# The third pass of a graph layer: rows on GpSimd, squares split between two engines, the copy a step later

## The chip, the cores and the metric

The kernel runs on one core of a Trainium2 chip. Its engines work in parallel, each through its own list of instructions in order: TensorE (PE in the profile; PEld is its loading of weights), VectorE (DVE), ScalarE (ACT), GpSimd (POOL), and SyncE (SP), which only issues transfers here. Semaphores order the engines among each other. The metric is the time of one execution on the device in microseconds (us); the time given is the median of several runs.

## The reference

Two layers follow each other on 16 graphs of 1024 nodes with 128 features. Layer 0 is a gated graph network of four steps, added to its input and normalized. Layer 1 thins out the adjacency matrix row by row, passes three times over all graphs, and joins what the passes leave:

```python
def _sage(x, adj, Wr, Wx, b, mf):
    deg = jnp.clip(jnp.sum(adj, axis=-1, keepdims=True), 1.0, None)
    agg = jnp.einsum('bij,bjd->bid', adj, x) / deg
    out = agg @ Wr + x @ Wx + b
    nrm = jnp.maximum(jnp.linalg.norm(out, axis=-1, keepdims=True), NORM_EPS)
    return out / nrm * mf[..., None]
...
h1 = _bn(jax.nn.relu(_sage(x, adj_d, Wr1, Wx1, b1, mf)), g1, be1)
h2 = _bn(jax.nn.relu(_sage(h1, adj_d, Wr2, Wx2, b2, mf)), g2, be2)
h3 = _bn(jax.nn.relu(_sage(h2, adj_d, Wr3, Wx3, b3, mf)), g3, be3)
xc = jnp.concatenate([h1, h2, h3], axis=-1) * mf[..., None]
return (xc @ Wl + bl) * mf[..., None]
```

`_bn` normalizes each feature over all nodes of all graphs, so a pass has to end before the next can use its result. The change lies in the third pass: `out` for `h3`, its row norm, the division, the mask and `relu`, and the sums of squares that `_bn` needs.

## The kernel before

The first stages (gated network, thinning, first and second pass) are outside the change. When the third pass starts, the aggregates `agg` of `h2` are already in memory (`s_ag`), and so are the turned rows of `h2` (`s_rt`); the third pass has no large matrix product any more.

`Sage.third` (L1850) goes through 32 units: 16 graphs, two halves `f` of 512 nodes each. A unit holds four blocks of 128 nodes by 128 features. The order of every engine's list is written out by hand (`manual_schedule`): what the loop emits first stands first in its engine's list. Step `i` of the loop emits work of several units, so that engines need not wait for each other within a step:

- SyncE: at the first half of each graph, `load_layer` for the next graph: 512 KB of aggregates (`q_agi`), 512 KB of turned rows (`q_xt`), and a small `s_rho`; three buffers each.
- TensorE: `out_next` of unit i (L1769): four products into `q_oa` (aggregates by weights), four into `q_ob` (rows by two weight matrices side by side), four small ones that add the bias. Then `turned` of unit i-3 (L1422): four transposes of the rows `s_r` into a PSUM tile `s_tr`. All three PSUM tiles have two buffers, which fills the PSUM.
- VectorE: `rows` of unit i-2 (L1407): lower bound, reciprocal and mask on a 128x4 tile of norms `ss`, then one 128x512 instruction, `max(o, 0) * ss`, into `s_r`. Then `bn_stats` of unit i-4 on `r3`. Then, of unit i, the add of `q_ob` into `s_o` (L1396), and the add of the other half of `q_ob` into `s_acc` (L1889).
- ScalarE, all of unit i but the last: four scalings of `q_oa` by the reciprocal degrees into `s_o` (L1393), four squares with an accumulator that gives each row's sum of squares (L1403, each followed by a read of the accumulator), a square root (L1404), and the copy of unit i-3's turned block from PSUM into `r3` (L1891).

Within a step, the squares read what the add on VectorE wrote, and that add reads what the scaling on ScalarE wrote. `s_o`, `s_r` and the loaded tiles have three buffers, `ss` has four.

At the start of step 8 stands `flagged` (L1995): VectorE reduces a table of checks (`bad`, 128x161) to a column, TensorE multiplies that by a column of ones into a PSUM tile taken from `s_tr`, and VectorE compares the product with 0.5. All of it stands ahead of step 8's own work in each list. At step 16 the flag is loaded into a register. It decides, after the whole pass, whether a slow general version has to run.

The third pass is followed by small matrices (`head_weights`) and the last pass, which normalizes and stores.

Of the kernel before, what the change touches and what calls it, by code (L numbers as in the profile page):

```python
# [8 lines left out]
F32 = mybir.dt.float32  # L9
BF = mybir.dt.bfloat16  # L10
# [4 lines left out]
AF = mybir.ActivationFunctionType  # L15
ALU = mybir.AluOpType
# [5 lines left out]
P = 128  # L22
B = 16
N = 1024
C = 128
# [340 lines left out]
class Norm:  # L366
# [5 lines left out]
    def __call__(self, out, rows):  # L372
        nc = self.nc
        st = self.pool.tile([P, NB, 6], F32, name="ln_st")
        mv = self.pool.tile([P, NB, 2], F32, name="ln_mv")
        for k in range(NB):
            nc.vector.bn_stats(st[:, k, :], rows[:, k, :])
        for k in range(NB):
            nc.vector.bn_aggr(mv[:, k, :], st[:, k, :])
        rs = self.pool.tile([P, NB], F32, name="ln_rs")  # L380
        nc.scalar.activation(rs, mv[:, :, 1], AF.Sqrt, bias=self.eps)
        nc.vector.reciprocal(rs, rs)
        for k in range(NB):
            nc.vector.tensor_scalar(out[:, k, :], rows[:, k, :], mv[:, k, 0:1], rs[:, k:k + 1],
                                    op0=ALU.subtract, op1=ALU.mult)


def sage_layers(ctx, tc, cst, adj, mask, not_r, summed, x1, W, vec, Wl, bl, out):
# [37 lines left out]
    def transposed(src, n, evac):  # L426
# [6 lines left out]
        return dst  # L433

    def sage(l, b, rows, ht, at, rd, mf, stats, psa, pso):

        pa = [psa.tile([C, HF], F32, name=f"s_a{f}") for f in range(2)]
# [57 lines left out]
    with ExitStack() as c1:  # L495
# [7 lines left out]
        for b in range(B):  # L503
# [36 lines left out]
            for f in range(2):  # L540
                nc.sync.dma_start(adj_t[b][4 * f:4 * f + 4].rearrange("k p n -> p k n"), at4[f])
            mf = row_tile("s_mf", mask[b])
            sage(0, b, rows, ht, at, rd, mf, stats, psa, pso)
        affine = batch_norm(0, stats)

# [85 lines left out]
class FixPoint:  # L631
# [206 lines left out]
    class Block:  # L838
# [22 lines left out]
        def rows(self, g):  # L861
            fix, nc = self.fix, self.fix.nc
            w = fix.wide.tile([P, N], BF, name="f_w", bufs=2)
            nc.vector.tensor_scalar(w, self.us[g], self.q[:, 2, g:g + 1], 0.5, op0=ALU.not_equal, op1=ALU.subtract)
            nr = fix.wide.tile([P, N], BF, name="f_nr", bufs=5)
            nc.vector.tensor_mul(nr, w, self.a[g])
            nc.sync.dma_start(fix.not_r[self.b0 + g, self.k * P:(self.k + 1) * P, :], nr)
            fix.read_last(self.i, g, nr)
# [341 lines left out]
class Sage:  # L1210
# [188 lines left out]
    def squares(self, o):  # L1399
# [4 lines left out]
        self.nc.scalar.activation(ss, ss, AF.Sqrt)  # L1404
        return ss

    def rows(self, b, f, o, ss):  # L1407
        nc = self.nc
        nc.vector.tensor_scalar(ss, ss, 1e-12, None, op0=ALU.max)  # L1409
        nc.vector.reciprocal(ss, ss)  # L1410
        nc.vector.tensor_mul(ss, ss, self.cst["mask"][:, 4 * f:4 * f + 4, b])
        r = self.wk.tile([P, 4, C], F32, name="s_r")
        sc = ss.rearrange("p (k o) -> p k o", o=1).to_broadcast([P, 4, C])
        nc.vector.scalar_tensor_tensor(r, o, 0.0, sc, op0=ALU.max, op1=ALU.mult)
        return r

    def split(self, f, src, hi, lo, c0=0):
# [363 lines left out]
            nc.tensor.matmul(pb[:, i, 0, :], g["rho"][:, blk], self.r6, start=False, stop=(i % 2 == 1))  # L1781
        g["oa", f], g["ob", f] = pa, pb

    def chain(self, b, f, scalar=False):

        g = self.g[b]
        pb = g.pop(("ob", f))
        g["o", f] = self.scale_rows(b, f, g.pop(("oa", f)), pb[:, :, 0, :], scalar)
        g["ss", f] = self.squares(g["o", f])
        return pb[:, :, 1, :]  # L1790

# [58 lines left out]
    def third(self):  # L1850

        nc, tc = self.nc, self.tc
        with ExitStack() as c:
            pool = lambda name, **k: c.enter_context(tc.tile_pool(name=name, **k))
            self.wk = pool("t_wk", bufs=3)
            self.ps2 = pool("t_ps2", bufs=2, space=PSUM)
            c.enter_context(tc.manual_schedule(engines={ET.PE, ET.DVE, ET.Activation, ET.Pool, ET.SP}))
            last, self.g = self.g[B - 1], {0: self.begun}
            nc.sync.dma_start(self.rt[B - 1, 1], last["rt", 1])
            for f in range(2):  # L1860
                nc.sync.dma_start(self.ag[B - 1, f], last["ag", f])
            units = [(b, f) for b in range(B) for f in range(2)]
            for i in range(len(units) + 4):
                if i == 8:
                    pt = self.ps2.tile([P, 4, P], F32, name="s_tr")
                    flag = flagged(nc, self.one, pt[:1, 0, :1], self.bad)
                if i == 16:
                    self.flag = nc.values_load(flag[0:1, 0:1], min_val=0, max_val=1,
                                               skip_runtime_bounds_check_because="0 or 1 by is_gt")

                if i < len(units):
                    b, f = units[i]
                    if f == 0 and b + 1 < B:
                        self.load_layer(b + 1)
                    self.out_next(b, f, self.ps2)
                if 3 <= i < len(units) + 3:
                    b2, f2 = units[i - 3]
                    pt = self.turned(self.g[b2].pop(("r", f2)), self.ps2)
                if 2 <= i < len(units) + 2:
                    b1, f1 = units[i - 2]  # L1880
                    g = self.g[b1]
                    g["r", f1] = self.rows(b1, f1, g.pop(("o", f1)), g.pop(("ss", f1)))
                if i >= 4:
                    b3, f3 = units[i - 4]
                    nc.vector.bn_stats(self.stats[2][:, 2 * b3 + f3, :], self.r3[:, b3, f3, :])
                if i < len(units):
                    pp = self.chain(b, f, True)
                    acc = self.acc[:, b, 4 * f:4 * f + 4, :]
                    nc.vector.tensor_add(acc, pp, acc)  # L1889
                if 3 <= i < len(units) + 3:  # L1890
                    nc.scalar.copy(self.r3[:, b2, f2, :], pt)  # L1891


    def last(self, r48):
# [97 lines left out]
    nc.vector.scalar_tensor_tensor(junk, a, 0.0, a, op0=ALU.is_gt, op1=ALU.not_equal, accum_out=bad[:, c:c + 1])  # L1992


def flagged(nc, wk, pt, bad):  # L1995

    t = wk.tile([P, 1], F32, name="l_max")
    nc.vector.tensor_reduce(t, bad, axis=AX.X, op=ALU.max)
    nc.vector.tensor_scalar(t, t, 0.0, None, op0=ALU.not_equal)
    col = wk.tile([P, 1], F32, name="l_col")  # L2000
    nc.vector.memset(col, 1.0)
    nc.tensor.matmul(pt, t, col, start=True, stop=True)
    f = wk.tile([1, 1], I32, name="l_flag")
    nc.vector.tensor_scalar(f, pt, 0.5, None, op0=ALU.is_gt)
    return f
# [72 lines left out]
```

## Time and profile before

| what | us |
|---|---|
| median of 3 runs | 2189.92 (2189.5 to 2190.53) |
| the profiled execution | 2193.03 |
| its span, first to last instruction | 2191.1 |
| third pass, first matmul to last `bn_stats` | 1988.22 to 2119.43 |
| in it, from the first to the last add into `s_o` | 1991.49 to 2112.13 = 120.64 |
| busy in those 120.64: TensorE, VectorE, ScalarE, GpSimd | 109.32, 93.19, 91.92, 0.00 |

Lines of the profile name an engine, a line of the kernel (L1396), an operation, the tiles written and read (out<-in), and their shapes. A line of the timeline gives start and duration in us, the number of merged instructions after x, and in brackets the idle time of the engine before it and what ended that. A group of the page gives busy time in all, mean duration in ns, and idle time before the group. An instruction's record can begin before its predecessor's ends; the distance between two starts ("pitch") is then less than the duration.

### The profile page before, as it was taken

How to read it: one execution, taken by the hardware profiler on the slowest of the kernel's cores; microseconds unless marked ns; L12 is line 12 of the kernel's file. 1: busy time of each engine (PE TensorE's matmuls, PEld its weight loads, DVE VectorE, ACT ScalarE, POOL GpSimd, SP SyncE). 2: the span in 40 equal slices, each digit the busy share in tenths (PEclk: the TensorE clock that was granted, in tenths of full speed). 3: DMA queues.
4: the chain of work that ended last, by engine and by line, in shares of the span. 5: the costliest groups of instructions: out<-in, count | busy, mean ns of one | idle time of the engine just before them, and what ended most of it. 6: DMA issues, size and time to landing. Idle time of an engine off the chain costs nothing. (4 is left out here: it accounts for less than half of the span.)

```text
span 2191.1 us, 32979 instructions
## 1 busy us (share of the span) xinstructions
PE 2068.8 (94%) x10217; PEld 1441.4 (66%) x10217; DVE 1838.4 (84%) x4215; ACT 1326.7 (61%) x3238; POOL 1240.4 (57%) x1226
## 2 busy tenths in 40 slices
PE   6999999999999999999999979999999899998977
PEld 4666556666556665556665557777777678887866
DVE  4898998989998889988989978888888767766878
ACT  3657557565666656656575566666666445555757
POOL 4458558467566476575585447777777445551002
PEclk9999999999999999999999989999999999999989
DMA  8348446456455276474383259888888577765505
GB/s 256 76 96 252 90 121 224 86 154 192 92 177 166 77 205 146 97 226 109 83 261 92 68 200 334 306 301 304 302 306 298 178 268 264 268 230 175 156 21 156
DMA packets 233853, 406.13 MB, mean 185 GB/s; under 512 B 79042, under 2 KB 100196, under 8 KB 233668
## 3 DMA queue, kind: packets, MB, share of 16 engines
q1 hardware_dynamic: 187844, 284.37, 39.9%
q0 software_dynamic: 41472, 117.46, 20.2%
q10 hardware_dynamic: 4352, 2.11, 0.4%
q8 instruction: 83, 1.36, 0.3%
q14 instruction: 102, 0.84, 0.1%
HBM read 313.48 MB, written 109.25 MB: 193 GB/s over the span
## 5 line engine op out<-in xcount | busy, mean ns | idle before, releaser
L1104 PE MATMUL h_g<-h_h,h_wh 128*128 128x512 f32 x768 | 396.0, 597 | 3.3 <-DVE h_r L1116 3.3
L1104 PE MATMUL h_g<-h_ms,h_wi 128*128 128x512 f32 x768 | 392.2, 592 | 0.0
L1123 POOL TENSOR_TENSOR h_zh<-h_r,h_h 128x512 f32<-128x512 f32 x126 | 175.4, 1392 | 258.9 <-ACT h_r L1119 255.8
L737 DVE TENSOR_TENSOR_SCAN f_rank<-f_a,f_first,f_pd 128x1024 f16<-128x1024 bf16 x128 | 299.4, 2345 | 4.2
L1092 PE MATMUL h_g<-h_a,h_hi 128*128 128x512 f32 x1024 | 278.8, 413 | 1.3 <-DMA h_a<-in_adj_dram 1.2
L1104 PEld LDWEIGHTS h_g<-h_ms,h_wi 128*128 128x128 f32 x768 | 145.5, 190 | 184.3 <-issue 169.4
L1511 POOL CAST p_b<-p_at 128x512 uint8<-128x512 f32 x256 | 219.7, 880 | 82.8 <-DVE p_at L1503 52.3
L1092 PE MATMUL h_g<-h_a,h_lo 128*128 128x512 f32 x1024 | 262.0, 393 | 0.2 <-DVE h_lo L1030 0.2
L1092 PEld LDWEIGHTS h_g<-h_a,h_hi 128*128 128x128 f32 x1024 | 190.1, 188 | 62.2 <-issue 21.8
L1403 ACT ACTIVATE s_junk<-s_o 128x128 bf16<-128x128 f32 x384 | 114.0, 298 | 169.2 <-DVE s_o L1396 158.3
L1092 PEld LDWEIGHTS h_g<-h_a,h_lo 128*128 128x128 f32 x1024 | 189.7, 188 | 39.0 <-DVE h_lo L1030 1.0
L1104 PEld LDWEIGHTS h_g<-h_h,h_wh 128*128 128x128 f32 x768 | 133.3, 190 | 100.3 <-issue 73.4
L1125 POOL TENSOR_TENSOR h_h<-h_h,h_zh 128x512 f32<-128x512 f32 x126 | 179.0, 1420 | 9.9
L1119 ACT ACTIVATE h_r<-h_r,h_bi 128x512 f32<-128x512 f32 x128 | 92.4, 722 | 151.5 <-DVE h_r L1118 151.4
L1124 POOL TENSOR_TENSOR h_zh<-h_z,h_zh 128x512 f32<-128x512 f32 x126 | 162.5, 1290 | 9.9
L1095 ACT COPY h_ms<-h_g 128x512 f32<-128x512 f32 x128 | 73.9, 577 | 149.7 <-PE h_g L1092 149.6
L910 ACT ACTIVATE f_u<-f_rank,f_q 128x128 f16<-128x128 f16 (+7 forms) x128 | 110.6, 867 | 69.4 <-DVE f_rank L850 69.4
L1778 PE MATMUL q_ob<-s_wxp,q_xt 128*128 128x256 f32 x512 | 125.3, 389 | 3.5 <-DVE s_ss L1409 2.1
L1992 DVE SCALAR_TENSOR_TENSOR p_junk<-p_a 128x1024 bf16<-128x1024 f32 x96 | 126.0, 1312 | 0.0
L887 ACT ACTIVATE f_pd<-f_rank,f_q 128x128 f32<-128x128 f16 x128 | 59.1, 462 | 98.7 <-DVE f_q L701 95.5
L1503 DVE SCALAR_TENSOR_TENSOR p_at<-p_nr,p_u 128x128 fp32r<-128x128 bf16 (+1 forms) x192 | 102.0, 543 | 18.0 <-ACT p_at L1495 14.6
L778 POOL TENSOR_SCALAR_AFFINE_SELECT f_both<-f_both 128x512 bf16<-128x512 bf16 x32 | 20.5, 642 | 165.1 <-DVE f_both L777 165.1
(264 smaller groups left out, 4807.8 us busy)
## 6 DMA issues: line engine op xcount, KB each, us to landing
h_a<-in_adj_dram POOLq DMA_DIRECT2D x128, 512.0 KB, 9.2
p_a<-in_adj_dram SPq DMA_DIRECT2D x96, 512.0 KB
f_a<-in_adj_dram POOLq DMA_DIRECT2D x128, 256.0 KB, 6.5
e_nr<-f_nr SPq DMA_DIRECT2D x128, 256.0 KB
p_nr<-e_nr SPq DMA_DIRECT2D x32, 1024.0 KB
h_test<-in_adj_dram SPq DMA_DIRECT2D x32, 512.0 KB
s_at<-p_b SPq DMA_DIRECT2D x32, 512.0 KB
s_ag<-s_ag SPq DMA_DIRECT2D x64, 256.0 KB
```

Source lines behind the costliest of these rows:

```text
L737: nc.vector.tensor_tensor_scan(out, a, other[:, 0, 0:1].to_broadcast([P, N]), start, op0=ALU.add, op1=ALU.bypass)
L910: nc.scalar.activation(u[:, :n1], rank[:, g, :n1], AF.Abs, bias=q[:, 1, g:g + 1], scale=q[:, 0, g:g + 1])
L1092: nc.tensor.matmul(pm[f], part[:, j, :], st.adj[j][:, half[f]], start=(j == 0 and n == 0), stop=(j == NB - 1 and n == 1))
L1104: nc.tensor.matmul(pg, lhs, rhs, start=(i == 0), stop=(i == len(mm) - 1))
L1123: aid.tensor_tensor(d, r, h, ALU.subtract)
L1124: aid.tensor_tensor(d, z, d, ALU.mult)
L1125: aid.tensor_tensor(h, h, d, ALU.add)
L1403: self.nc.scalar.activation(junk, o[:, i, :], AF.Square, accum_out=ss[:, i:i + 1])
L1503: self.nc.vector.scalar_tensor_tensor(g["at"][:, j, c0:c0 + low], v[:, j, c0:c0 + low], 0.0, pu[:, :low], op0=ALU.is_lt, op1=ALU.is_lt)
L1511: self.nc.gpsimd.tensor_copy(g["b", f][:, j, :], g["at"][:, j, f * HF:(f + 1) * HF].bitcast(F32))
L1778: nc.tensor.matmul(pb[:, i], g["xt"][:, f, blk], self.wxp, start=(i % 2 == 0), stop=False)
L1992: nc.vector.scalar_tensor_tensor(junk, a, 0.0, a, op0=ALU.is_gt, op1=ALU.not_equal, accum_out=bad[:, c:c + 1])
```

## The change

Six things change, all in `third` and its helpers.

1. `rows_by_pool`: the product of `rows` goes from one VectorE instruction to four GpSimd instructions of 128x128, `max(o * ss, 0)`. The three small instructions stay on VectorE. For the last two units `rows` is kept.
2. `shared_squares`: of the four squares, two stay on ScalarE, and two go to VectorE, as products of a tile with itself with an accumulator. They stand behind the add into `s_o` and ahead of the add into `s_acc`. Each pair of sums has its own 128x2 tile, and its own square root on ScalarE, so two roots instead of one.
3. The copy of the turned block is that of the step before (unit i-4), and it stands between ScalarE's scaling and its squares, no longer behind the root.
4. `bn_stats` is accordingly that of unit i-5, and the loop has one step more at its end.
5. The flag: the reduction of `bad` (`any_bad`) stands in step 8 behind the add into `s_o`, the matmul in step 10 behind the transposes, the compare (`flagged`) in step 11. The register is loaded at step 16 as before.
6. The multiplication by `ss` is now ahead of the maximum with zero; `ss` is not negative.

```diff
+    def shared_squares(self, o):
+        nc, small = self.nc, self.small
+        sa, sv = [small.tile([P, 2], F32, name=f"s_ss{i}") for i in range(2)]
+        for i in range(2):
+            junk = small.tile([P, C], BF, name="s_junk")
+            nc.scalar.activation(junk, o[:, i, :], AF.Square, accum_out=sa[:, i:i + 1])
+        for i in range(2):
+            junk = small.tile([P, C], BF, name="s_junk2")
+            nc.vector.scalar_tensor_tensor(junk, o[:, i + 2, :], 1.0, o[:, i + 2, :], op0=ALU.mult, op1=ALU.mult,
+                                           accum_out=sv[:, i:i + 1])
+        ss = small.tile([P, 4], F32, name="s_ss", bufs=4)
+        for i, t in enumerate((sa, sv)):
+            nc.scalar.activation(ss[:, 2 * i:2 * i + 2], t, AF.Sqrt)
+        return ss
...
+    def rows_by_pool(self, b, f, o, ss):
+        nc = self.nc
+        nc.vector.tensor_scalar(ss, ss, 1e-12, None, op0=ALU.max)
+        nc.vector.reciprocal(ss, ss)
+        nc.vector.tensor_mul(ss, ss, self.cst["mask"][:, 4 * f:4 * f + 4, b])
+        r = self.wk.tile([P, 4, C], F32, name="s_r")
+        for i in range(4):
+            nc.gpsimd.tensor_scalar(r[:, i, :], o[:, i, :], ss[:, i:i + 1], 0.0, op0=ALU.mult, op1=ALU.max)
         return r
...
-            for i in range(len(units) + 4):
-                if i == 8:
-                    pt = self.ps2.tile([P, 4, P], F32, name="s_tr")
-                    flag = flagged(nc, self.one, pt[:1, 0, :1], self.bad)
+            pts = {}
+            for i in range(len(units) + 5):
...
-                    pt = self.turned(self.g[b2].pop(("r", f2)), self.ps2)
+                    pts[i] = self.turned(self.g[b2].pop(("r", f2)), self.ps2)
                 if 2 <= i < len(units) + 2:
                     b1, f1 = units[i - 2]
                     g = self.g[b1]
-                    g["r", f1] = self.rows(b1, f1, g.pop(("o", f1)), g.pop(("ss", f1)))
-                if i >= 4:
-                    b3, f3 = units[i - 4]
+                    rows = self.rows_by_pool if i < len(units) else self.rows
+                    g["r", f1] = rows(b1, f1, g.pop(("o", f1)), g.pop(("ss", f1)))
+                if i >= 5:
+                    b3, f3 = units[i - 5]
                     nc.vector.bn_stats(self.stats[2][:, 2 * b3 + f3, :], self.r3[:, b3, f3, :])
                 if i < len(units):
-                    pp = self.chain(b, f, True)
+                    g = self.g[b]
+                    pb = g.pop(("ob", f))
+                    g["o", f] = self.scale_rows(b, f, g.pop(("oa", f)), pb[:, :, 0, :], True)
+                if 4 <= i < len(units) + 4:
+                    b4, f4 = units[i - 4]
+                    nc.scalar.copy(self.r3[:, b4, f4, :], pts.pop(i - 1))
+                if i == 8:
+                    col = any_bad(nc, self.one, self.bad)
+                if i == 10:
+                    pt = self.ps2.tile([P, 4, P], F32, name="s_tr")[:1, 0, :1]
+                    nc.tensor.matmul(pt, *col, start=True, stop=True)
+                if i == 11:
+                    flag = flagged(nc, self.one, pt)
+                if i < len(units):
+                    g["ss", f] = self.shared_squares(g["o", f])
                     acc = self.acc[:, b, 4 * f:4 * f + 4, :]
-                    nc.vector.tensor_add(acc, pp, acc)
-                if 3 <= i < len(units) + 3:
-                    nc.scalar.copy(self.r3[:, b2, f2, :], pt)
+                    nc.vector.tensor_add(acc, pb[:, :, 1, :], acc)
...
-def flagged(nc, wk, pt, bad):
+def any_bad(nc, wk, bad):
     t = wk.tile([P, 1], F32, name="l_max")
     nc.vector.tensor_reduce(t, bad, axis=AX.X, op=ALU.max)
     nc.vector.tensor_scalar(t, t, 0.0, None, op0=ALU.not_equal)
     col = wk.tile([P, 1], F32, name="l_col")
     nc.vector.memset(col, 1.0)
-    nc.tensor.matmul(pt, t, col, start=True, stop=True)
+    return t, col
+
+
+def flagged(nc, wk, pt):
     f = wk.tile([1, 1], I32, name="l_flag")
     nc.vector.tensor_scalar(f, pt, 0.5, None, op0=ALU.is_gt)
     return f
```

More of the change, by code (lines that the diff above doesn't have):

```diff
@@ L1414, in rows @@
         nc.vector.scalar_tensor_tensor(r, o, 0.0, sc, op0=ALU.max, op1=ALU.mult)
+        return r
+    def rows_by_pool(self, b, f, o, ss):
[6 more added lines that the diff above has]
+            nc.gpsimd.tensor_scalar(r[:, i, :], o[:, i, :], ss[:, i:i + 1], 0.0, op0=ALU.mult, op1=ALU.max)
         return r
@@ L1782, in out_next, with chain @@
         g["oa", f], g["ob", f] = pa, pb
-    def chain(self, b, f, scalar=False):
+    def chain(self, b, f):
         g = self.g[b]
         pb = g.pop(("ob", f))
-        g["o", f] = self.scale_rows(b, f, g.pop(("oa", f)), pb[:, :, 0, :], scalar)
+        g["o", f] = self.scale_rows(b, f, g.pop(("oa", f)), pb[:, :, 0, :])
         g["ss", f] = self.squares(g["o", f])
```

## The prediction

> **What bounds the kernel now.** I read the page's slices first (TensorE 90% or more through nearly the whole span), then the page's groups, then the timeline of each engine through the third pass, the only stage that is edited. It runs from the first matmul at 1988.22 to the last `bn_stats` at 2119.43 us. The page points at ScalarE's squares, which wait for VectorE's add into `s_o`:
>
> ```profile
> L1403 ACT ACTIVATE s_junk<-s_o 128x128 bf16<-128x128 f32 x384 | 114.0, 298 | 169.2 <-DVE s_o L1396 158.3
> ```
>
> One step of ScalarE (timeline: start, duration, operation):
>
> ```profile
> 2007.39 0.57 ACT L1891 COPY s_r<-s_tr 128x512 f32<-128x512 f32 x1
> 2007.86 1.15 ACT L1393 ACTIVATE s_o<-q_oa,s_rdeg 128x128 f32<-128x128 f32 x4
> 2009.77 0.31 ACT L1403 ACTIVATE s_junk<-s_o 128x128 bf16<-128x128 f32 x1 [0.76 <-DVE s_o L1396]
> ...
> 2011.08 0.21 ACT L1404 ACTIVATE s_ss<-s_ss 128x4 f32<-128x4 f32 x1
> 2011.19 0.57 ACT L1891 COPY s_r<-s_tr 128x512 f32<-128x512 f32 x1
> ```
>
> Copy to copy is 3.80 us (3.79 in the steps that follow): copy 0.47, scale 1.15, 0.76 of waiting for the add, squares and root 1.42. ScalarE is the loop; VectorE waits for it twice a step (0.35 before the add, 0.24 before `bn_stats`). TensorE in the same steps:
>
> ```profile
> 2006.86 1.06 PE L1775 MATMUL q_oa<-s_wr,q_agi 128*128 128x128 f32 x8
> 2010.15 1.06 PE L1775 MATMUL q_oa<-s_wr,q_agi 128*128 128x128 f32 x8
> ...
> 2018.49 0.19 PE L2002 MATMUL s_tr<-l_col,l_max 128*1 128x1 f32 x2 [4.89 <-DVE l_col L2001]
> 2018.61 2.08 PE L1775 MATMUL q_oa<-s_wr,q_agi 128*128 128x128 f32 x8
> 2020.48 3.62 PE L1778 MATMUL q_ob<-s_wxp,q_xt 128*128 128x256 f32 x8
> ```
>
> While it may run ahead, TensorE needs 3.29 a step: that is the floor under any shortening of ScalarE. The flag's matmul, put between steps 7 and 8, makes TensorE wait 4.89 us; the next matmuls take twice their time (2.08 for 1.06; the granted clock in that stretch is 0.53). VectorE's adds around it stand at 2016.63 and 2024.58, 7.95 apart: the flag costs 7.95 - 3.79 = 4.16 us.
>
> The last rows are those of GpSimd, idle through the third pass before:
>
> ```profile
> 1779.91 1.28 POOL L1420 TENSOR_TENSOR q_rl<-s_r,q_rh 128x512 fp32r<-128x512 f32 x1 [6.38 <-ACT q_rh L1419]
> ```
> ```profile
> 1780.04 1.70 DVE L1414 SCALAR_TENSOR_TENSOR s_r<-s_o,s_ss 128x512 f32<-128x512 f32 x1
> 1788.87 0.69 DVE L1414 SCALAR_TENSOR_TENSOR s_r<-s_o,s_ss 128x512 f32<-128x512 f32 x1
> 214.57 1.64 DVE L866 TENSOR_TENSOR f_nr<-f_w,f_a 128x1024 bf16<-128x1024 bf16 x1
> 216.13 1.49 DVE L864 TENSOR_SCALAR f_w<-f_u,f_q 128x1024 bf16<-128x1024 f16 x1
> ```
> ```profile
> 214.32 1.34 POOL L1124 TENSOR_TENSOR h_zh<-h_z,h_zh 128x512 f32<-128x512 f32 x1
> 215.74 1.60 POOL L1125 TENSOR_TENSOR h_h<-h_h,h_zh 128x512 f32<-128x512 f32 x1
> ```
>
> A VectorE instruction that reads two SBUF operands takes 0.69 alone and 1.70 if a GpSimd instruction is under way: it ends 0.55 after that one's end, so it waited for nearly all of it. At 214 us the engines take turns: a pending GpSimd instruction goes in between two of VectorE's. Adds with an operand in PSUM (691 to 693 ns in all three passes) and `bn_stats` show no such delay.
>
> **ScalarE, part by part.** Two of four squares go: the pitch of one is 0.30, so -0.60. A second root adds 0.11 of pitch. The copy moves into the 0.76 wait, so its 0.47 leaves the sum. ScalarE's step becomes 1.15 scale, 0.76 (copy inside), 0.73 two squares, 0.22 two roots: 2.9. The second root also waits for VectorE's squares, on time or up to 0.2 late (below). ScalarE is no longer the bound.
>
> **VectorE and GpSimd.** The 128x512 product (0.69, pitch 0.60) leaves VectorE; two 128x128 squares with an accumulator come. The exact form exists once (L1296, both inputs the same tile): 278 ns, the next instruction 0.21 later, its accumulator read beside it. VectorE's step without contention: three small ones 0.60, `bn_stats` 0.61, add 0.73 (the square needs its end), squares 2 x 0.21, add into `s_acc` 0.60: 2.96. GpSimd gets four 128x128 f32 instructions with a per-partition scalar. L1948 has that form with two scalars: 446 to 453 ns, pitch 0.44. L1906 (bfloat16) has 0.60, the other end; I take 0.45, the row with the same types.
>
> Their order: with VectorE's step starting at 0, the small ones end at 0.57, GpSimd starts at 0.67 (0.10 from a VectorE end to a GpSimd start, at 2135.19) and ends at 0.67 + 3 x 0.44 + 0.45 = 2.45. The add ends at 1.90; the first square is ready at 1.94, with GpSimd's third instruction ending at 2.0 and the fourth to come. By the rows, a blocked instruction of 0.69 ends 0.55 behind the GpSimd one, so one of 0.28 ends 0.13 behind. If the fourth goes first: first square to 2.58, second to 2.79, add into `s_acc` from 2.72, next step at 3.32. If a square slips between: 3.2. Free of any contention: 2.96; both squares held for a whole 0.45 and none of it overlapped: 2.96 + 2 x 0.45 = 3.86, which the rows make unlikely, as a held instruction overlaps 0.15 of the wait. With 0.30 each it is 3.56. Against TensorE's floor of 3.29 I take **T = 3.32**.
>
> The Trainium skill (SBUF — State Buffer, section "SBUF: two separate sides") says that the ports VectorE and GpSimd share are an exclusive lock, held for a whole instruction, and that a VectorE instruction with two SBUF inputs takes part. By that rule T is 3.32, without it 3.29; the trace agrees, with the 1.70 for 0.69 above.
>
> **Queues and waits.** TensorE: the transposes of step i wait for GpSimd's rows of step i-1. Those are done 2.45 after that step's start; TensorE, which may start step i only after the add into `s_acc` of step i-2, needs 2.85 before it gets there: covered, and with GpSimd at 0.55 an instruction no longer. The copy comes a step later, so TensorE's second `s_tr` buffer is freed one scale into the step before, ahead of need. `s_o` has three buffers: the scale now waits for GpSimd's rows three units back, done at 2.45 against a scale at 2.9; cover 0.45. SP issues loads in the same order and only sooner; a graph's 1 MB in 6.6 us is 159 GB/s where the start of this pass shows 297. Nothing else is in GpSimd's queue until the last pass.
>
> **Flag.** Its three VectorE instructions at step 8 take 0.55 in front of the squares, the compare at step 11 0.15; the matmul at step 10 runs 0.2 and asks for a buffer whose copy is in the same step, as do the next transposes: 0 to 0.3. With the register load's hiccup at 2053 us (0.2 to 0.3, kept) I take 0.9 for all, between 0.5 and 5 (stall and slow clock back).
>
> **Ends.** Steps 0 to 4 become TensorE's: their matmuls never waited for ScalarE, so the add of step 4 can start 0.19 after 2003.29, at 2003.48 (before: 2005.24). The tail: the last two rows stay on VectorE, behind squares (+0.4) and the add (0.6) but with an earlier root; rows 31 end 4.5 us after the last add instead of 4.03: +0.5.
>
> **Sum.** The add of step 31 stood at 2112.13. After: 2003.48 + 27 T + 0.9, and 0.5 in the tail. Gain = 2112.13 - 2003.48 - 1.4 - 27 T = 107.25 - 27 T; with T = 3.32 it is 17.6 us. The profiled execution took 2193.03 (span 2191.1), 3.1 above the median of 2189.92; from the median I predict **2172.3**, a profile of this kind 2175.4. The last pass is not changed.
>
> **Rivals.**
> 1. *Contention makes VectorE the bound*: T = 3.56, gain 11.1, 2178.8. For it: the take-turns rows. Against: GpSimd has one instruction left when the squares arrive. 0.17.
> 2. *GpSimd's price, the slower side*. By the order above T = 1.54 + 4p, p being one GpSimd instruction. At p = 0.60 (L1906) T is 3.94 and the time 2189.0, no change; it breaks even at p = 0.61, is 0.2% slower from 0.65, and with 0.70 the time is 2199.9. Against: L1948 is 0.45 in all 17 cases, with VectorE busy beside it. 0.09 for slower, 0.05 for about equal. The Trainium skill (GPSIMD Engine Reference, section "4.1 Engine selection") advises VectorE over GpSimd for such elementwise work; the trace has 0.45 against 0.28 (L1336 alone), dearer but here beside other work.
> 3. *The flag's stall returns* at steps 10 to 11, with the slow clock: +4.1 on the sum, 2176.4. 0.05.
>
> **How the numbers follow.** The forecast, T from 3.29 (2171.5) to 3.45 (2175.8), has 0.64. The low end, 2169.5, allows 2 us for the flag and tail costing nothing; the high end, 2180.5, takes in rival 1 and a little of its unknown. What is left out is p above 0.53 and luck. Faster by over 0.2% (4.4 us, about what a measurement can tell): 0.64 + 0.17 + 0.05 = 0.86; within 0.05; slower 0.09.
>
> **What would show it.** TensorE's matmuls into `q_oa` 3.3 us apart without idle time; GpSimd's rows at 0.45; VectorE's squares 0.28 or, held, 0.4 to 0.7; ScalarE waiting for TensorE or VectorE, not filling the step; no 4.89 us gap. I am wrong if GpSimd's rows take 0.6, or if adds are 3.6 apart.

## The result, and the profile after

The changed kernel takes 2173.95 us (median of six runs, 2172.15 to 2178.44), the kernel before 2189.91 (2189.5 to 2197.4): a ratio of 0.9926, with an interval of 0.9914 to 0.9938. That is 0.7% faster, and 1.7 us above the predicted 2172.3. The profiled execution took 2176.16 (span 2174.3), 16.87 less than that of before, where 17.6 was forecast.

| third pass, us | before | forecast | after |
|---|---|---|---|
| first to fifth add into `s_o` (steps 0 to 3) | 13.75 | 11.99 | 12.42 |
| fifth to last add | 106.89 | 27 x 3.32 + 0.9 = 90.54 | 91.49 |
| in it, mean of the steps 12 to 30 | 3.81 | 3.32 | 3.344 |
| start of the last add to end of the last `bn_stats` | 7.30 | 7.80 | 7.52 |
| sum | 127.94 | 110.33 | 111.43 |

So the pass gives 16.5 of the 16.87 us, and no other stage is needed to explain the result. The mean of 3.344 hides a pattern: in the second half the steps alternate between 2.99 and 3.68, which sum to 6.67. ScalarE's timeline after (start, duration, operation, and in brackets the idle time before it with what ended that):

```profile
2060.14 1.14 ACT L1393 ACTIVATE s_o<-q_oa,s_rdeg 128x128 f32<-128x128 f32 x4
2061.15 0.60 ACT L1916 COPY s_r<-s_tr 128x512 f32<-128x512 f32 x1
2062.09 0.31 ACT L1412 ACTIVATE s_junk<-s_o 128x128 bf16<-128x128 f32 x1 [0.34 <-DVE s_o L1396]
...
2062.82 0.30 ACT L1419 ACTIVATE s_ss<-s_ss 128x2 f32<-128x2 f32 x2
2063.82 1.14 ACT L1393 ACTIVATE s_o<-q_oa,s_rdeg 128x128 f32<-128x128 f32 x4 [0.70 <-POOL s_r L1439]
2064.83 0.60 ACT L1916 COPY s_r<-s_tr 128x512 f32<-128x512 f32 x1
```

The copy now lies in the wait for the add, which leaves 0.34 of the 0.76. ScalarE has time left, as forecast; but every second scaling waits 0.70 for GpSimd's rows, which the forecast had "done at 2.45 against a scale at 2.9". GpSimd's timeline, and its instruction over the whole pass (minimum, median and maximum duration in ns):

```profile
2060.85 5.92 POOL L1439 TENSOR_SCALAR s_r<-s_o,s_ss 128x128 f32<-128x128 f32 x8 [0.80 <-PE s_tr L1450]
2067.57 3.70 POOL L1439 TENSOR_SCALAR s_r<-s_o,s_ss 128x128 f32<-128x128 f32 x5 [0.80 <-PE s_tr L1450]
```
```profile
L1439 POOL TENSOR_SCALAR s_r<-s_o,s_ss x120: 700/712/930, 1996.3 to 2096.4; 128x128 f32<-128x128 f32 x120
```

One row instruction takes 0.71 us, not 0.45. The four of a unit take 2.89 of a step of 3.34 (median, from the first start to the last end), two units run without a pause (x8), and in the second half GpSimd, idle before, is busy for 30.50 of 35.00 us (2055 to 2090). VectorE beside it:

```profile
2058.33 0.69 DVE L1396 TENSOR_TENSOR s_o<-q_ob,s_o 128x512 f32<-128x512 f32 x1 [0.75 <-ACT s_o L1393]
...
2061.37 0.69 DVE L1396 TENSOR_TENSOR s_o<-q_ob,s_o 128x512 f32<-128x512 f32 x1
2062.09 0.29 DVE L1415 SCALAR_TENSOR_TENSOR s_junk<-s_o 128x128 bf16<-128x128 f32 x1
...
2062.31 0.29 DVE L1415 SCALAR_TENSOR_TENSOR s_junk<-s_o 128x128 bf16<-128x128 f32 x1
...
2065.05 0.69 DVE L1396 TENSOR_TENSOR s_o<-q_ob,s_o 128x512 f32<-128x512 f32 x1 [0.75 <-ACT s_o L1393]
...
2066.81 0.15 DVE L1434 TENSOR_SCALAR s_ss<-s_ss 128x4 f32<-128x4 f32 x1
```

These lines close the loop that sets 6.67 for two steps. TensorE does not set it: its starts stay 3.29 apart there (below), and it is busy for all 35.00 us. `s_o` has three buffers, so the scaling of unit i+2 needs the rows of unit i-1 done. From the scaling at 2063.82 the way goes over the add (2065.05), VectorE's squares and its add into `s_acc`, the small instructions of unit i-1 (2066.81), GpSimd's four rows from 2067.57 (0.19 after the last small instruction ended at 2067.38; the bracket names PE, whose transposes were long done), and so to the next scaling that waits, at 2070.5. The scaling between the two finds its buffer free, and its step is the short one. The squares start 0.03 behind the add in spite of the GpSimd instruction under way, and take 0.29: they are not held until it ends.

TensorE, in the flag's steps and later:

```profile
2024.36 0.19 PE L1921 MATMUL s_tr<-l_col,l_max 128*1 128x1 f32 x2 [1.32 <-ACT s_r L1916]
2024.47 1.16 PE L1800 MATMUL q_oa<-s_wr,q_agi 128*128 128x128 f32 x8
...
2057.64 1.06 PE L1800 MATMUL q_oa<-s_wr,q_agi 128*128 128x128 f32 x8
2060.93 1.06 PE L1800 MATMUL q_oa<-s_wr,q_agi 128*128 128x128 f32 x8
```

The pause of 4.89 is down to 1.32 (its matmul now waits for the buffer that the copy frees), and the next matmuls take 1.16, not 2.08; the granted clock behind it is 1.00 (2024.36 to 2027.60), where it was 0.53 before. Steps 8 to 11 take 14.37 together, 1.2 above four of 3.29.

### The profile page after: what moved, and what is told of

It reads as the page before. It is cut to its first block, busy times and chain, and to the rows that moved or that the text cites. A ratio compares the mean times of both kernels' runs of the same rounds, so it can differ in the third digit from the quotient of the medians.

```text
span 2174.3 us, 33161 instructions
## 1 busy us (share of the span) xinstructions
PE 2063.3 (95%) x10217; PEld 1438.1 (66%) x10217; DVE 1831.1 (84%) x4313; ACT 1312.8 (60%) x3142; POOL 1324.3 (61%) x1346
## 5 line engine op out<-in xcount | busy, mean ns | idle before, releaser
L1403 ACT ACTIVATE s_junk<-s_o 128x128 bf16<-128x128 f32 x256 | 76.1, 298 | 141.6 <-DVE s_o L1396 141.6
```

## Experiments

The forecast had the new time from three parts: the copy in ScalarE's wait, the engine moves (rows to GpSimd, two squares to VectorE), and the flag. Two views had to be told apart. By the first the parts overlap, because each ends at TensorE's floor of 3.29, and the copy alone would reach it. By the second ScalarE and VectorE both have to be relieved. Beside the times, the length of the pass from the first to the last add decides here: two executions of one kernel give it within 0.05 us (103.91 and 103.95 for the changed kernel; 101.32 and 101.31 for the one with a fourth buffer), while the whole time of one kernel spreads over up to 8 us (2187.62 to 2195.71 for the kernel before). Part of that arises ahead of the pass: its first add stands at 1989.78 in one profile of the kernel with a fourth buffer and at 1991.85 in the other.

**The flag alone.** The kernel before, with the flag's three parts in steps 8, 10 and 11, and nothing else:

```diff
-                if i == 8:
-                    pt = self.ps2.tile([P, 4, P], F32, name="s_tr")
-                    flag = flagged(nc, self.one, pt[:1, 0, :1], self.bad)
...
+                if i == 8:
+                    col = any_bad(nc, self.one, self.bad)
+                if i == 10:
+                    pf = self.ps2.tile([P, 4, P], F32, name="s_tr")[:1, 0, :1]
+                    nc.tensor.matmul(pf, *col, start=True, stop=True)
+                if i == 11:
+                    flag = flagged(nc, self.one, pf)
```

> The kernel before with the flag alone in steps (reduction in step 8 behind the add, matmul in step 10, compare in step 11). Theory M (parts overlap): ScalarE stays the loop at 3.79 us a step, the 4.16 us that the flag cost go except for at most 0.5, so 3.6 to 4.2 us faster than before, about 2186. Rival R1 (the stall only moves: the flag's matmul waits for an s_tr buffer and TensorE pauses over 3 us again, with the slow clock): 0 to 1 us faster. Adds into s_o 3.79 apart in both, but one gap of 7 to 8 us under R1.

Measured: 2187.06 against 2191.23 for before on the same chip, 0.9983 (0.9974 to 0.9993); the pass is 116.59, 4.05 shorter, and its later steps 3.81 as before. TensorE in it:

```profile
2026.19 0.19 PE L1891 MATMUL s_tr<-l_col,l_max 128*1 128x1 f32 x2 [2.10 <-ACT s_r L1899]
2026.31 1.86 PE L1775 MATMUL q_oa<-s_wr,q_agi 128*128 128x128 f32 x8
2027.97 2.90 PE L1778 MATMUL q_ob<-s_wxp,q_xt 128*128 128x256 f32 x8
```

TensorE still pauses for 2.10, and the matmuls after that are slow (2.90 for 1.89; the granted clock from 2026.19 to 2030.90 is 0.64). That hardly costs anything here: of the steps 8 to 11, one takes 3.98 and the others 3.79, in which TensorE has 0.5 to spare. The flag is worth nearly its 4.16 by itself.

**The copy and the flag, no engine moved.** The changed kernel, with the rows and the squares back where they were:

```diff
-                    rows = self.rows_by_pool if i < len(units) else self.rows
+                    rows = self.rows
...
-                    g["ss", f] = self.shared_squares(g["o", f])
+                    g["ss", f] = self.squares(g["o", f])
```

> The changed kernel with rows back on VectorE in one instruction and all four squares back on ScalarE: only the copy's place and the flag differ from before. Theory M: the copy's 0.47 us goes into the 0.76 us wait, ScalarE's step is 1.15 + 0.76 + 1.42 = 3.33 us, VectorE's sum 3.0 to 3.1; against TensorE's floor of 3.29 nothing more is to be had, so the step is 3.33 to 3.36 and the time within 2 us of the changed kernel, 15 to 18 us faster than before. Rival R2 (each part brings its own share, so most of the gain comes from the work that left ScalarE and VectorE): step 3.6 or more, at most 9 us faster than before. If VectorE's waits bind: 3.45, 13 us faster.

Measured: 2174.13, 0.9925 (0.9908 to 0.9943) of before; the pass is 104.14. That is the whole gain of the change, as far as the runs can tell: the medians are 0.2 us apart, the passes 0.2, and the interval of the ratio is nearly 8 us wide. Nearly every step is 3.30. ScalarE in it:

```profile
2074.34 0.60 ACT L1916 COPY s_r<-s_tr 128x512 f32<-128x512 f32 x1
2075.22 0.31 ACT L1403 ACTIVATE s_junk<-s_o 128x128 bf16<-128x128 f32 x1 [0.28 <-DVE s_o L1396]
...
2076.53 0.20 ACT L1404 ACTIVATE s_ss<-s_ss 128x4 f32<-128x4 f32 x1
2076.64 1.12 ACT L1393 ACTIVATE s_o<-q_oa,s_rdeg 128x128 f32<-128x128 f32 x4
2077.64 0.60 ACT L1916 COPY s_r<-s_tr 128x512 f32<-128x512 f32 x1
```

The prediction's own terms say it: 3.79 less 0.47 for the copy is 3.32, and TensorE cannot go below 3.29. The 0.5 that the moved squares take from ScalarE on top buys nothing in the changed kernel.

**The engine moves and the flag, the copy left at the end of the step.**

```diff
-            for i in range(len(units) + 5):
+            for i in range(len(units) + 4):
...
-                if i >= 5:
-                    b3, f3 = units[i - 5]
+                if i >= 4:
+                    b3, f3 = units[i - 4]
...
-                if 4 <= i < len(units) + 4:
-                    b4, f4 = units[i - 4]
-                    nc.scalar.copy(self.r3[:, b4, f4, :], pts.pop(i - 1))
...
+                if 3 <= i < len(units) + 3:
+                    nc.scalar.copy(self.r3[:, b2, f2, :], pts.pop(i))
```

> The changed kernel with the copy back at its old place behind the roots (rows on GpSimd, two squares on VectorE, flag in steps stay). Theory M: ScalarE's step is 1.15 + 0.76 + 0.73 + 0.22 + 0.47 = 3.33 us and GpSimd's loop through the s_o buffers 3.34, so 3.34 to 3.45 a step, and within 3 us of the changed kernel, 13 to 17 us faster than before. Rival R2 (the parts add up): the copy's 0.47 a step is missing, step 3.8, 4 to 5 us faster than before.

Measured: 2175.47, 0.9934 (0.9917 to 0.995); the pass is 104.85, its steps mostly 3.35 with some of 3.48 to 3.51 between (3.38 on average from step 17 on). ScalarE:

```profile
2071.90 0.57 ACT L1926 COPY s_r<-s_tr 128x512 f32<-128x512 f32 x1
2072.50 1.14 ACT L1393 ACTIVATE s_o<-q_oa,s_rdeg 128x128 f32<-128x128 f32 x4
2074.45 0.31 ACT L1412 ACTIVATE s_junk<-s_o 128x128 bf16<-128x128 f32 x1 [0.81 <-DVE s_o L1396]
2075.38 0.57 ACT L1926 COPY s_r<-s_tr 128x512 f32<-128x512 f32 x1
```

Here ScalarE is the loop: copy 0.47, scale 1.15, wait 0.81, squares and roots 0.93, in all 3.36. Either of the two parts is enough to come within 0.1 us of TensorE's 3.29, so they overlap; they do not add up.

**The squares split, the rows back on VectorE.** Of the changed kernel only the line of the rows is undone:

```diff
-                    rows = self.rows_by_pool if i < len(units) else self.rows
+                    rows = self.rows
```

> The changed kernel with rows back on VectorE (squares split, copy moved, flag in steps stay). Theory M: VectorE becomes the bound with 0.60 + 0.60 + 0.61 + 0.73 + 0.42 + 0.60 = 3.56 us a step, 27 x 0.22 = 6 us slower than the changed kernel, 10 to 11 us faster than before. Rival R3 (GpSimd's instructions, 0.71 each, hold the changed kernel back, so that without them it is faster): step at TensorE's 3.29, 1 to 2 us faster than the changed kernel.

Measured: 2179.9, 0.9949 (0.9933 to 0.9966); the pass is 108.42, every later step 3.56 but the one in which the flag is loaded (3.65). VectorE, whose lines carry no idle time any more:

```profile
2070.86 0.67 DVE L1396 TENSOR_TENSOR s_o<-q_ob,s_o 128x512 f32<-128x512 f32 x1
...
2073.21 0.69 DVE L1429 SCALAR_TENSOR_TENSOR s_r<-s_o,s_ss 128x512 f32<-128x512 f32 x1
...
2074.42 0.67 DVE L1396 TENSOR_TENSOR s_o<-q_ob,s_o 128x512 f32<-128x512 f32 x1
```

The 2.96 of the prediction plus the 0.60 of the row product are 3.56: VectorE binds. So the squares on VectorE make the pass 4.3 longer than leaving them on ScalarE (104.14), and the rows on GpSimd pay that back. The two moves need each other, and together they give what the copy alone gives.

**What the GpSimd instruction costs.** The four row instructions in four forms:

```diff
+        self.r6z = const([P, 1], 0.0, "s_zero")
...
-        for i in range(4):
-            nc.gpsimd.tensor_scalar(r[:, i, :], o[:, i, :], ss[:, i:i + 1], 0.0, op0=ALU.mult, op1=ALU.max)
+        z = self.r6z
+        nc.gpsimd.tensor_scalar(r[:, 0, :], o[:, 0, :], ss[:, 0:1], 0.0, op0=ALU.mult, op1=ALU.max)
+        nc.gpsimd.tensor_scalar(r[:, 1, :], o[:, 1, :], 0.0, ss[:, 1:2], op0=ALU.max, op1=ALU.mult)
+        nc.gpsimd.tensor_scalar(r[:, 2, :], o[:, 2, :], ss[:, 2:3], z, op0=ALU.mult, op1=ALU.max)
+        nc.gpsimd.tensor_scalar(r[:, 3, :], o[:, 3, :], ss[:, 3:4], 0.0, op0=ALU.mult, op1=ALU.add)
```

> The changed kernel with four forms of GpSimd's row instruction, one for each of the four blocks: (1) as it is, times a pointer scalar, then maximum with the immediate 0; (2) maximum with the immediate first, then times the pointer; (3) times the pointer, then maximum with a pointer to zeros; (4) times the pointer, then plus the immediate 0 (this leaves relu out of every fourth block). It asks why the form takes 0.71 us where the last pass's (times a pointer, plus a pointer) takes 0.45. Theory F1 (the maximum is dear): forms 1 to 3 near 0.71, form 4 at 0.45. Theory F2 (the immediate is dear): form 3 at 0.45, the others near 0.71. Theory F3 (VectorE's work beside it is what stretches it): all four alike, near 0.71.

```profile
L1440 POOL TENSOR_SCALAR s_r<-s_o,s_ss x30: 709/710/711, 1994.0 to 2089.7; 128x128 f32<-128x128 f32 x30
L1441 POOL TENSOR_SCALAR s_r<-s_o,s_ss x30: 714/725/727, 1994.8 to 2090.4; 128x128 f32<-128x128 f32 x30
L1442 POOL TENSOR_SCALAR s_r<-s_o,s_ss,s_zero x30: 792/798/995, 1995.5 to 2091.1; 128x128 f32<-128x128 f32 x30
L1443 POOL TENSOR_SCALAR s_r<-s_o,s_ss x30: 362/368/506, 1996.2 to 2092.0; 128x128 f32<-128x128 f32 x30
```

The maximum makes it dear, wherever it stands: 710 to 798 ns with it, 368 with a sum in its place (450 had been expected). The row that the price was taken from (the last pass, `mult` and then `add`) is 442 in the changed kernel too; it had the types and the shape, not the operation. With one of the four made cheap two steps take 6.58 and the pass is 101.69; its one execution took 2170.2. By their medians the four take 2.60 instead of 2.85 (4 x 0.712), and that 0.25 is more than the loop through `s_o` needs: 6.67 for two steps was only 0.09 above 2 x 3.29. The steps still alternate here, 3.43 and 3.15 in these lines, though their sum is TensorE's and every second add waits for TensorE:

```profile
2060.76 0.69 DVE L1397 TENSOR_TENSOR s_o<-q_ob,s_o 128x512 f32<-128x512 f32 x1 [0.51 <-PE s_tr L1454]
...
2063.91 0.69 DVE L1397 TENSOR_TENSOR s_o<-q_ob,s_o 128x512 f32<-128x512 f32 x1
...
2067.34 0.69 DVE L1397 TENSOR_TENSOR s_o<-q_ob,s_o 128x512 f32<-128x512 f32 x1 [0.51 <-PE s_tr L1454]
```

So steps that alternate do not yet show that the loop costs time; the sum of two does.

**A fourth buffer for `s_o`.**

```diff
-        o = self.wk.tile([P, 4, C], F32, name="s_o")
+        o = self.wk.tile([P, 4, C], F32, name="s_o", bufs=4 if scalar else None)
```

> The changed kernel with four buffers of s_o instead of three in the third pass. Theory S1: the loop that binds its second half goes over GpSimd's rows, the release of their s_o buffer, the scale three units later, the add, the small instructions and the next rows, 6.67 us for two steps; with a fourth buffer the steps are TensorE's 3.29 and even, no longer 2.99 and 3.68 in turn, and the time is 0.5 to 1.5 us less. Theory S2 (GpSimd itself or VectorE binds): steps stay at 3.34 on average, same time. The profile tells the two apart, the time hardly.

Measured: 2171.53, 0.9905 (0.9888 to 0.9923); the pass is 101.32, 2.6 shorter, and every later step is 3.29 but the two at the register load (3.66 and 3.11). The gain was expected at 0.5 to 1.5, from the second half alone, which gives 0.7; 0.5 come from steps 0 to 3 (11.93 for 12.42), 0.4 from steps 4 to 7 and 0.8 from steps 8 to 11. VectorE's adds, now paced by TensorE:

```profile
2061.50 0.69 DVE L1396 TENSOR_TENSOR s_o<-q_ob,s_o 128x512 f32<-128x512 f32 x1 [0.22 <-PE s_tr L1450]
...
2064.79 0.69 DVE L1396 TENSOR_TENSOR s_o<-q_ob,s_o 128x512 f32<-128x512 f32 x1 [0.36 <-PE s_tr L1450]
...
2068.08 0.69 DVE L1396 TENSOR_TENSOR s_o<-q_ob,s_o 128x512 f32<-128x512 f32 x1 [0.23 <-PE s_tr L1450]
```

The alternation is gone with GpSimd's price unchanged at 0.71. So it is the loop through three buffers that binds the changed kernel, not GpSimd's throughput and not contention on VectorE. TensorE's pause of 1.32 at the flag is gone too:

```profile
2021.69 0.19 PE L1921 MATMUL s_tr<-l_col,l_max 128*1 128x1 f32 x2
2021.81 1.16 PE L1800 MATMUL q_oa<-s_wr,q_agi 128*128 128x128 f32 x8
```

So in the changed kernel the pause comes from the same loop, which makes the copies late. Steps 8 to 11 now take 13.55, 0.39 above four of 3.29.

**Is 3.29 TensorE's floor?** The kernel with the fourth buffer, its four small bias products left out:

```diff
-            nc.tensor.matmul(pb[:, i], g["xt"][:, f, blk], self.wxp, start=(i % 2 == 0), stop=False)
-        for i in range(4):
+            nc.tensor.matmul(pb[:, i], g["xt"][:, f, blk], self.wxp, start=(i % 2 == 0),
+                             stop=(ps is self.ps2 and i % 2 == 1))
+        for i in range(0 if ps is self.ps2 else 4):
```

> The four-buffer kernel without the four bias matmuls of the third pass (the bias row is left out of its result, about 0.23 us a step on TensorE; loads stay). Theory M (TensorE's 3.29 is the floor under all versions): TensorE's step is 3.06, VectorE's 2.96 and GpSimd's 2.8 to 3.0 are next, so 3.06 to 3.15 a step and 4 to 7 us faster than the four-buffer kernel. Rival R4 (another engine or the loops among them hold it at 3.3): within 1 us of the four-buffer kernel.

Measured: 2167.51 against 2171.53 with them, on the same chip; the pass is 95.17, 6.15 shorter, and every later step is 3.06 but the two at the register load (3.66 and 2.88). In the profiled pair the whole gains only 2.4, since this pass also starts 1.5 later. TensorE:

```profile
2062.10 1.06 PE L1800 MATMUL q_oa<-s_wr,q_agi 128*128 128x128 f32 x8
2065.16 1.06 PE L1800 MATMUL q_oa<-s_wr,q_agi 128*128 128x128 f32 x8
```

With less on TensorE the step falls by 0.23, which is what the four products take of its line (2022.00 to 2022.22 in the changed kernel): TensorE binds the four-buffer kernel at 3.29.

**The flag early.** The kernel with copy and flag alone, the flag's parts at steps 0, 2 and 3:

```diff
-                if i == 8:
+                if i == 0:
...
-                if i == 10:
+                if i == 2:
...
-                if i == 11:
+                if i == 3:
```

> Copy moved and flag in steps, rows and squares as before the change, and the flag three steps into the pass instead of eight (reduction in step 0, matmul in step 2, compare in step 3), when no transposes use the s_tr buffers. Theory M: steps 3.30, and the 0.5 + 0.3 us that steps 10 and 11 lost go, so 0.5 to 1 us faster than the kernel with copy and flag alone, about 17.5 us faster than before, within 2 us of the changed kernel. Rival: the reduction in step 0 delays the first steps by as much, no difference.

Measured: 2173.11, 0.9914 (0.9897 to 0.9932); the pass is 103.20, 0.94 shorter than with steps 8, 10 and 11. All steps are 3.30 but one: step 15 to 16, in which the flag goes into registers, is 4.13. The load costs 0.83 here; the forecast had 0.2 to 0.3 for it, from the kernel before (4.08 for 3.80), where ScalarE is the loop as well. ScalarE at the load, in the kernel before and in this one:

```profile
2053.28 0.57 ACT L1891 COPY s_r<-s_tr 128x512 f32<-128x512 f32 x1
2054.03 1.14 ACT L1393 ACTIVATE s_o<-q_oa,s_rdeg 128x128 f32<-128x128 f32 x4 [0.19 <-issue]
```
```profile
2041.43 1.14 ACT L1393 ACTIVATE s_o<-q_oa,s_rdeg 128x128 f32<-128x128 f32 x4 [0.71 <-DVE s_r L1429]
```

Before, the copy of 0.57 stood directly ahead of the load and ScalarE was idle for 0.19 behind it; now a root of 0.20 stands there and it is idle for 0.71. That the load runs beside the copy would explain it, but no run tests that. With the fourth buffer and the early flag (below) the step is 3.65 and the next one 2.94, together two of 3.29: there the load costs nothing in the end.

**Repeats, and the best of it together.** The changed kernel and the one with a fourth buffer once more, beside a kernel with the fourth buffer and the early flag:

```diff
-        o = self.wk.tile([P, 4, C], F32, name="s_o")
+        o = self.wk.tile([P, 4, C], F32, name="s_o", bufs=4 if scalar else None)
...
-                if i == 8:
+                if i == 0:
...
-                if i == 10:
+                if i == 2:
...
-                if i == 11:
+                if i == 3:
```

> The changed kernel once more, to stand on one chip with the next two. 15 to 18 us faster than before; adds into s_o 2.99 and 3.68 us apart in turn in the second half.

> The changed kernel with four s_o buffers once more, on the same chip. Theory S1: 1 to 2.5 us faster than the changed kernel (0.045 us a step over 27 steps, and 1 us at steps 8 to 11, where the three-buffer kernel had gaps of 3.4 to 3.8). Theory S2 (what was seen on different chips was the chips): no difference.

> Four s_o buffers, and the flag in steps 0, 2 and 3. Theory: TensorE's 3.29 in every step but where the register is loaded, 0.3 to 0.8 us below the four-buffer kernel, some 20 us faster than before: faster than both kernels of the case.

| | time, us | ratio to before, interval | pass | mean of steps 12 to 30 |
|---|---|---|---|---|
| changed kernel | 2176.69 | 0.9928 (0.9914 to 0.9941) | 103.95 | 3.347 |
| fourth buffer | 2173.04 | 0.9911 (0.9898 to 0.9925) | 101.31 | 3.299 |
| fourth buffer, early flag | 2171.79 | 0.9916 (0.9903 to 0.993) | 101.01 | 3.29 |

TensorE in the last one, with no pause ahead of the flag's matmul:

```profile
1995.19 0.19 PE L1921 MATMUL s_tr<-l_col,l_max 128*1 128x1 f32 x2
1995.31 1.16 PE L1800 MATMUL q_oa<-s_wr,q_agi 128*128 128x128 f32 x8
```

The pass repeats to 0.05 us, so the 2.6 us of the fourth buffer are real there. In the whole time the medians are 3.7 and 4.9 us lower than the changed kernel's, while the intervals overlap: that it is faster as a whole is likely, not shown.

The fourth buffer also gives the engine moves a use. With copy and early flag alone the pass is 103.20, with the moves and a fourth buffer as well 101.01: 2.2 less, 1.0 of it in steps 0 to 3 and 0.8 at the register load. No run has the fourth buffer without the moves, so its share is open.

**Are VectorE's squares held by a long GpSimd instruction?** In the changed kernel the squares start at odd moments of a GpSimd instruction. One instruction of 128x512 in place of four (with one factor for all four blocks) puts them inside a long one:

```diff
-        for i in range(4):
-            nc.gpsimd.tensor_scalar(r[:, i, :], o[:, i, :], ss[:, i:i + 1], 0.0, op0=ALU.mult, op1=ALU.max)
+        nc.gpsimd.tensor_scalar(r, o, ss[:, 0:1], 0.0, op0=ALU.mult, op1=ALU.max)
```

> The changed kernel with GpSimd's four row instructions replaced by one of 128x512 that scales all four blocks by the first block's factor (three blocks in four are scaled wrongly). It asks how long a GpSimd instruction keeps VectorE's squares waiting. Theory K1 (only while it reads its input, a length that grows with the elements): squares that start inside it end up to 0.6 us or more late, where the 128x128 ones kept them 0.17 at most. Theory K2 (a fixed time at its start): at most 0.17 again.

```profile
L1438 POOL TENSOR_SCALAR s_r<-s_o,s_ss x30: 1990/1996/1997, 1996.5 to 2091.4; 128x512 f32<-128x512 f32 x30
```
```profile
L1415 DVE SCALAR_TENSOR_TENSOR s_junk<-s_o x64: 283/291/293, 1991.7 to 2093.1; 128x128 bf16<-128x128 f32 x64
```

None of the 64 squares is held, though 58 of them meet an instruction of 2.0 us; all of those started at least 0.94 after its beginning. That excludes a lock for a whole instruction of this kind. It does not tell whether the ports are taken for the first part of an instruction or only at its start: for that a square would have had to start in the first 0.9 us, and none did. Its one execution took 2172.57, with a pass of 101.14: four rows in one go take 2.0 and not 2.89, and the loop through `s_o` has room again.

## Why the prediction came out right, and which of its steps were wrong

The time, the sign and the range held, in part by luck. Two of its steps were wrong and cancelled out: GpSimd's rows cost more than it said, and VectorE's squares do not wait for them as it said. By its own sign (rows that take 0.6) it was wrong about the mechanism on GpSimd. And one thing it had in its own numbers it did not say.

- **What bounds before, and TensorE's floor**: right. Moving the copy out of ScalarE's loop gives 3.30; in the kernel with a fourth buffer, where TensorE sets 3.29, taking work from TensorE gives 3.06.
- **"ScalarE's step becomes ... 2.9"**: right as far as it goes, since ScalarE waits, 0.34 for the add and every second step 0.70 for GpSimd. What the prediction left out is that 3.79 - 0.47 = 3.32 is already at the floor. The gain was booked on the change as a whole; the run with the copy and the flag alone shows that with three buffers the engine moves add nothing measurable to it.
- **"I take 0.45, the row with the same types"**: wrong, 0.71. Neither end of its bounds (0.45 and 0.60) held it, because both rows were chosen by type and shape, and the operation decides: 368 ns with `add`, 710 with `max`.
- **"If the fourth goes first: first square to 2.58"**, and with it T = 1.54 + 4p: wrong too. By that formula 0.71 would have given 4.38 a step and 2201 us, 0.5% slower, which was rival 2. The formula makes the squares wait for the last GpSimd instruction. They do not: their median is 291 ns and their maximum 451, so at most 0.17 is lost. T came out at 3.344, next to 3.32, for another reason, the loop through `s_o`.
- **"With GpSimd at 0.55 an instruction no longer" covered**: did not come about. At 0.71 the rows hold TensorE's transposes up once in the pass, for 0.2; its one pause is the 1.32 at the flag.
- **"cover 0.45" in `s_o`**: this is what the higher price used up. Four instructions cost 4 x 0.26 = 1.04 more than forecast, the cover was 0.45, and the wait moved to ScalarE's scaling (0.70 in every second step). That it costs only 0.05 a step, 3.344 for 3.29, is the gift of the buffers: two units share the delay, and the loop is 6.67 long for two steps. The fourth buffer takes it away.
- **Rival 1, T = 3.56 by contention**: did not happen; the same 3.56 appears where the rows stay on VectorE, without any contention.
- **The flag, 0.9**: 1.2 measured at steps 8 to 11 of the changed kernel, and 0.14 at the register load (3.65 and 3.07 for two of 3.29). With the fourth buffer the same two places cost 0.39 and 0.19, so about 0.8 of the 1.2 belongs to the loop through `s_o` and the flag itself costs 0.6, less than forecast. Moving it is worth 4.05 alone, against the 4.16 that it cost.
- **Start and tail**: steps 0 to 3 took 12.42 for 11.99, in both profiles of the changed kernel, and 11.93 with the fourth buffer: the same loop again. The tail grew by 0.22 for a forecast 0.5. The 4.03 that the forecast took for the end of the last rows is their start (2116.16); they end 4.72 after the last add, and after the change 4.94.

On contention the prediction weighed a rule of the Trainium skill (SBUF — State Buffer, section "SBUF: two separate sides"), by which the shared ports are an exclusive lock for a whole instruction. This case's runs agree with it for the earlier passes' 128x512 GpSimd instructions (1.70 for 0.69) and not for this one: squares that start 0.3 to 0.6 into a GpSimd `tensor_scalar` of 0.71, or at least 0.94 into one of 2.0, run at their full speed. In the other order GpSimd does wait: every one of its row instructions that took over 0.73 in the changed kernel had a square under way when it began.

## What to carry to other kernels

When several parts of a change relieve the same loop, work out each part alone against the next floor before adding them up: here moving one copy by one step reached TensorE's 3.29 to within 0.01, and two moves between engines bought nothing on top as long as `s_o` had three buffers. Price an instruction on an engine by a row with the same operation, not only the same types and shape, and if there is none, put the bounds wider than the rows that differ from it. When an engine takes over a step between a buffer's writer and its release, count the whole loop through the buffers, over as many steps as there are buffers: short and long steps in turn point to it, their sum against the floor says whether it costs anything, and one more buffer shows it.

## What the runs showed of the hardware that was not expected

- On GpSimd a 128x128 f32 `tensor_scalar` takes 0.37 us with `mult` and `add` of a constant, 0.71 with `mult` and `max` of a constant in the same place, 0.80 if the zero is a per-partition operand. One 128x512 instruction with `max` takes 2.00, four of 128x128 take 2.78 to 3.00.
- VectorE and GpSimd collide only near the start of a GpSimd instruction of this kind. In the changed kernel 23 row instructions began while a square was under way and took 0.74 to 0.93 for 0.71. Four squares that started 0.12 to 0.18 into one took 0.39 to 0.45 for 0.29, and two at 0.25 took 0.36; those that started 0.29 to 0.6 into one took 0.28 to 0.29.
- Behind a pause of TensorE of 1.32 us (changed kernel) or 1.69 (copy and flag alone) the granted clock stayed at 1.00; the 1.16 for 1.06 of the next matmuls stands behind the flag's matmul without any pause too. Behind one of 2.10 (flag alone) it was 0.64, with matmuls of 1.86 and 2.90 for 1.06 and 1.89, and behind one of 4.89 (before) 0.53, with 2.08 and 3.62. Each is one profiled execution, and in that of 2.10 another pause of 0.64 stands 5 us ahead, so what length of pause it takes is not shown.
- Loading the flag into registers cost 0.83 us in the kernels with copy and flag alone, 0.28 in the kernel before, and nothing in the one with a fourth buffer and the early flag, which makes it up in the next step.
